# Layers 2 to 3 of a four-layer kernel: another order of the chains, moved gated adds, an earlier exp table, and seven spare products

## The chip, the cores and the metric

The kernel runs on one core of a Trainium2 chip. A core has five engines, each of which works through a queue of instructions of its own, in order: TensorE (PE in the profile; PEld is its weight loads), VectorE (DVE), ScalarE (ACT), GpSimd (POOL) and SyncE (SP, which here issues transfers). They meet through semaphores. The metric is the device time of one execution, in microseconds; lower is better. The profile calls a source line L477, for line 477 of the kernel.

## The reference, cut to what matters

Four layers work on a stream `x` of 4 x 256 tokens of 256 features. Each adds a gated cross attention to a small context and then a gated feed-forward part. The change lies where layer 2 ends and layer 3 begins:

```
x = x + tanh(g_xattn[2]) * L2_xattn(layernorm(x), ctx)     # 16 heads of 16, 64 keys, causal
x = x + tanh(g_ffn[2])   * L2_ffn(layernorm(x))            # int8-rounded x times int8-rounded weight
x = x + tanh(g_xattn[3]) * L3_xattn(layernorm(x), ctx)     # as in layer 2
x = x + tanh(g_ffn[3])   * L3_ffn(layernorm(x))            # shared experts + best 2 of 8

L2_ffn: x_max = max|x| of each token; x_scale = x_max/127; x_q = round(x/x_scale)
        y = (x_q @ w_q.T) * x_scale * w_scale + bias
attention: softmax(q k / 4, causal) v, then @ Wout.T
```

Everything is float32 but the rounded numbers, which are whole and go through TensorE as bfloat16.

## The kernel before, in words

`x` stays in SBUF as eight tiles of 128 tokens, `x[0]` to `x[7]`; tiles 0 to 3 are group 0, tiles 4 to 7 are group 1. Query products and feed-forward products take a group (512 tokens) at a time, softmax and its products a tile.

`layernorm(g)` takes the statistics of four tiles (`bn_stats` and `bn_aggr` on VectorE, L431 and L434), one square root on ScalarE (L436), a reciprocal on VectorE (L439), and scales the tiles: on VectorE (L450), or with `scalar=True` on ScalarE from a shift made at L443 (L447). The results come from the tag `xn` with seven buffers. `transposed` turns the four tiles on TensorE (L462) and copies the two halves out, one on ScalarE (L169) and one on VectorE (L171).

`attention23` is the attention of layers 2 and 3. `queries(g)` is normalisation, transposition and the query products (`mm2`, L477), which ScalarE scales into `xT` (L1034). It is run for group 0 first and, in steps, for group 1 beside the first tiles. For each tile, `scores` makes the products with the keys (L1048 for the causal mask in even tiles, L1058), the row maxima (L1071), the differences (L1073) and the exponentials (L1082); `weights` sums (L491), inverts (L492) and scales on GpSimd (L493); `attend` turns the weights (L507), copies them (L508), multiplies by the values (L1090), copies (L1099) and multiplies by the output weight (L1102). `in_flight` runs them as a pipeline: in iteration i the scores of tile i, the gated add of tile i-3, the weights of tile i-1 and `attend` of tile i-2. `gated_add` is one VectorE instruction, `x[t] = ps * gate + x[t]` (L512).

`ffn2` is the feed-forward part of layer 2. `rounded(g)` normalises a group on ScalarE, takes maxima (L1963), scales and rounds on VectorE (L1968, L1970), and adds the bias to `x` on GpSimd (L1974). `rounded(0)` is written into the last iterations of layer 2's attention. `ffn2` itself goes through the two groups: transposition (L1985), copies on ScalarE (L1986), products (L1991), then `y = ps * xs * scale` on VectorE (L1995) and `x[t] += y` on GpSimd (L1996). In the source `rounded(1)` comes ahead of group 0's products, and layer 3's `queries(0)` after all of `ffn2`.

The order of the work is not written out by hand. A planner takes the instructions by priority, which is the order of the source, and lays each engine's queue out beforehand from estimates of its own on when each would be ready; on the chip every engine then follows its queue. `behind(later, sooner)` forbids the planner to put one instruction ahead of another. Tiles of a tag share a number of buffers: `t4` has six of 4 KB, `xn` seven of 1 KB, `xT` two, the PSUM tag `mm` four.

ScalarE holds one table of functions at a time; square root and exponential need different ones, and a load (ACT_TABLE_LOAD in the profile) stands ahead of the first instruction that needs the other.

## Time and profile before

| what | value |
|---|---|
| median of 3 runs | 839.23 us (837.9 to 839.84) |
| the profiled execution, its own time | 837.3 us |
| its span, first to last instruction | 835.4 us |
| mean granted TensorE clock | 0.978 |
| busy: PE, DVE, ACT, POOL | 93%, 60%, 35%, 29% |
| layer 2's attention, first L1058 to end of last L1102 | 544.43 to 592.25 us |
| `ffn2`, first L1985 to end of last L1996 | 592.09 to 607.91 us |
| layer 3's attention, first L1058 to end of last L1102 | 615.53 to 661.34 us |

All times within the execution are microseconds from the start of its span. A busy TensorE is not one at its peak: matmuls overlap, and their ends are modelled. Idle time is given with the instruction that ended it.

### The profile page before, as it was taken

How to read it: one execution, taken by the hardware profiler on the slowest of the kernel's cores; microseconds unless marked ns; L12 is line 12 of the kernel's file. 1: busy time of each engine (PE TensorE's matmuls, PEld its weight loads, DVE VectorE, ACT ScalarE, POOL GpSimd, SP SyncE). 2: the span in 40 equal slices, each digit the busy share in tenths (PEclk: the TensorE clock that was granted, in tenths of full speed). 3: DMA queues.
4: the chain of work that ended last, by engine and by line, in shares of the span. 5: the costliest groups of instructions: out<-in, count | busy, mean ns of one | idle time of the engine just before them, and what ended most of it. 6: DMA issues, size and time to landing. Idle time of an engine off the chain costs nothing.

```text
span 835.4 us, 12470 instructions
## 1 busy us (share of the span) xinstructions
PE 772.9 (93%) x4492; PEld 519.2 (62%) x4492; DVE 497.3 (60%) x1146; ACT 291.6 (35%) x508; POOL 246.4 (29%) x211
## 2 busy tenths in 40 slices
PE   6999999898999999999999989998579899999993
PEld 4544443687575776676555746655236557999993
DVE  5565454874682554545879559788869664334320
ACT  2121112343312333322633477166455521233320
POOL 1355454322132343321031200024424203344222
PEclk9999999999999999999999999899789999999997
DMA  9510215700121253324900001800000102222223
GB/s 343 189 39 0 62 40 204 262 22 4 29 72 40 72 141 83 74 35 123 378 17 7 1 1 37 324 24 1 26 0 2 51 8 78 55 51 46 33 26 71
DMA packets 32740, 64.14 MB, mean 77 GB/s; under 512 B 5121, under 2 KB 19713, under 8 KB 31905
## 3 DMA queue, kind: packets, MB, share of 16 engines
q1 hardware_dynamic: 25216, 52.56, 18.2%
q0 software_dynamic: 7104, 9.93, 7.3%
q8 instruction: 39, 0.64, 0.3%
q10 hardware_dynamic: 352, 0.79, 0.3%
q14 instruction: 29, 0.23, 0.1%
HBM read 53.86 MB, written 10.45 MB: 77 GB/s over the span
## 4 chain that ended last, share of the span: by engine, by line
PE 51%; DVE 9%; ACT 4%; issue 1%; POOL 1%; DMA 0%; POOLq 0%; DVEq 0%; ACTq 0%
PE wide L1435 9%; PE wide L477 7%; PE mm L1451 4%; PE mm L1525 3%; PE mm L709 3%; PE mm L1899 3%; PE mm L1883 2%; PE wide L961 2%; PE wide L1562 2%; PE wide L1563 2%; PE mm L1774 2%; PE mm L477 2%; DVE sm L491 1%; PE mm L507 1%; PE mm L1102 1%; PE wide L1058 1%
## 5 line engine op out<-in xcount | busy, mean ns | idle before, releaser
L493 POOL TENSOR_TENSOR attn<-attn,sm 128x1024 f32<-128x1024 f32 x32 | 61.1, 1913 | 229.3 <-DVE sm L492 179.0
L477 PE MATMUL wide<-xT,big 128*128 128x512 f32 (+1 forms) x240 | 108.6, 600 | 1.1 <-DVE shared L1656 0.9
L737 DVE TENSOR_TENSOR rope<-wide,big 128x512 f32<-128x512 f32 x96 | 59.6, 682 | 52.0 <-PE wide L477 52.0
L477 PEld LDWEIGHTS wide<-xT,big 128*128 128x128 f32 (+1 forms) x240 | 43.4, 188 | 57.3 <-issue 49.3
L1435 PE MATMUL wide<-blk,still 128*128 128x128 f32 x640 | 74.8, 275 | 0.6 <-DVE blk L1407 0.6
L1435 PEld LDWEIGHTS wide<-blk,still 128*128 128x128 f32 x640 | 73.1, 192 | 0.8 <-issue 0.8
L709 PE MATMUL mm<-vo,attnT 128*128 128x256 f32 x256 | 58.6, 382 | 1.5 <-ACT attnT L508 1.5
L477 PE MATMUL wide<-xT,dense 128*128 128x512 f32 (+1 forms) x120 | 55.1, 599 | 0.0
L709 PEld LDWEIGHTS mm<-vo,attnT 128*128 128x128 f32 x256 | 47.8, 190 | 11.4 <-ACT attnT L508 3.2
L508 ACT COPY attnT<-mm 128x512 f32<-128x512 f32 x64 | 34.4, 587 | 46.2 <-PE mm L507 45.7
L491 DVE TENSOR_REDUCE sm<-attn 128x16 f32<-128x1024 f32 x32 | 38.7, 1208 | 15.2 <-ACT attn L485 13.8
L1397 DVE COPY still<-big 128x1024 f32 x20 | 13.9, 693 | 52.0 <-PE wide L1435 44.5
L1466 POOL DMA_INDIRECT sums<-ring,scratch x20 | 31.6, 1578 | 40.4 <-ACT ring L1462 18.8
L1466 POOL DMA_INDIRECT sums<-ring,big x17 | 27.0, 1591 | 48.5 <-ACT ring L1545 18.2
L507 PE MATMUL mm<-ident,attn 128*128 128x128 f32 x256 | 33.7, 275 | 5.7 <-POOL attn L493 5.7
L1370 POOL DMA_INDIRECT xs<-xd,scratch x20 | 20.0, 1002 | 62.3 <-PE mm L1404 34.0
L512 DVE SCALAR_TENSOR_TENSOR x<-mm,tg,x 128x256 f32<-128x256 f32 x44 | 20.5, 471 | 29.4 <-PE mm L709 18.2
L1451 PE MATMUL mm<-big,hidden 128*128 x160 | 37.7, 379 | 0.0
L507 PEld LDWEIGHTS mm<-ident,attn 128*128 128x128 f32 x256 | 29.1, 141 | 13.3 <-POOL attn L493 8.5
L1443 ACT ACTIVATE hidden<-wide 128x512 f32<-128x512 f32 x20 | 12.0, 599 | 72.8 <-PE wide L1435 67.5
L477 PEld LDWEIGHTS wide<-xT,dense 128*128 128x128 f32 (+1 forms) x120 | 21.5, 185 | 24.4 <-issue 22.7
L791 ACT COPY big<-mm 128x512 f32<-128x512 f32 x16 | 8.6, 589 | 68.0 <-PE mm L779 61.7
(359 smaller groups left out, 1572.1 us busy)
## 6 DMA issues: line engine op xcount, KB each, us to landing
big<-in_L_w_gate_up SPq DMA_DIRECT2D x8, 1024.0 KB, 12.1
big<-in_L_w_down SPq DMA_DIRECT2D x8, 512.0 KB, 8.9
w_L_qk<-in_L_qk SPq DMA_DIRECT2D x4, 896.0 KB
big<-in_L_w SPq DMA_DIRECT2D x2, 1480.0 KB, 7.9
big<-in_L_w SPq DMA_DIRECT2D x2, 1110.0 KB
big<-in_L_wo SPq DMA_DIRECT2D x1, 2048.0 KB
big<-in_L_w SPq DMA_DIRECT2D x2, 1024.0 KB, 5.3
xd<-xn SPq DMA_DIRECT2D x16, 128.0 KB, 1.8
```

Source lines behind the costliest of these rows:

```text
L477: nc.tensor.matmul(ps, w(c), xT[:, c, :], start=(c == 0), stop=(c == 1))
L491: nc.vector.tensor_reduce(sm, e, AX.X, ALU.add)
L493: nc.gpsimd.tensor_tensor(e, e, sm.unsqueeze(2).to_broadcast([P, groups, n]), ALU.mult)
L507: nc.tensor.transpose(ps[:, i * P : (i + 1) * P], ev[:, pr * P : (pr + 1) * P], ident)
L508: nc.scalar.copy(aT[:, half * 4 : half * 4 + 4, :].rearrange("p i t -> p (i t)"), ps)
L709: nc.tensor.matmul(ps[:, :D], aT[:, s, :], vo[:, s, :], start=(s == 0), stop=(s == NP - 1))
L737: nc.vector.tensor_tensor(m[:, s, :].rearrange("q (b t) -> q b t", t=S), ps[:, s, :].rearrange("q (b t) -> q b t", t=S), table, ALU.mult,)
L1435: nc.tensor.matmul(ps[:, k, f : f + P], w[:, at : at + P], st[:, c * P : (c + 1) * P], start=(c == 0), stop=(c == 1),)
L1451: nc.tensor.matmul(ps[:, :D], hT[:, j * P : (j + 1) * P], self.w[:, bass.ds(r + j * D, D)], start=(j == 0), stop=(j == n - 1),)
L1466: nc.gpsimd.indirect_dma_start(out=self.sums[b % len(self.sums)], out_offset=bass.IndirectOffsetOnAxis(ap=self.scatter[:, b : b + 1].bitca ...
L1525: nc.tensor.matmul(ps[:n, f : f + P], w[:, c * FU0 + f : c * FU0 + f + n], st[:, c * P : (c + 1) * P], start=(c == 0), stop=(c == 1),)
L1899: nc.tensor.matmul(ps[:, :D], terms[:, k, f, i * P : (i + 1) * P], w2[:, f, :], start=(f == 0 and k == 0), stop=(f == 7 and k == 2),)
```

## The change

- `ffn2` is written as `unit(g, xq, xs)`. Group 0's unit comes first; then seven products of `ident` with a weight of layer 3 (128x128 by 128x512, float32), whose result nothing reads, held behind group 0's last product; then layer 3's normalisation, transposition and query products of group 0; and only then `rounded(1)` and group 1's unit. `attention23` finds group 0's queries made.
- In layers 2 and 3, the gated adds of tiles 0 to 5 are a ScalarE multiplication into a tile of its own and a GpSimd add. Tiles 6 and 7 keep the VectorE instruction.
- In `attention23`, the table of the exponential is loaded right behind the square root of group 1.
- Layer 3's normalised tiles and the transposed rounded numbers come from the tag `t4` in place of `xn` and `xT`.

```
-    def layernorm(g, scalar=False, after=()):
+    def layernorm(g, scalar=False, after=(), into=None, table=None):
...
         made = nc.scalar.activation(rstd, mv[:, :, 1], AF.Sqrt, bias=eps)
         if after:
             behind(made, after[1])
+        if table is not None:
+            behind(nc.scalar.preload_act_table(table), made)
         nc.vector.reciprocal(rstd, rstd)
...
-            n = sb.tile([P, D], F32, tag="xn", name="xn", bufs=AHEAD + 2)
+            n = sb.tile([P, D], F32, tag="xn", name="xn", bufs=AHEAD + 2) if into is None else into[:, i, :]
...
-    def in_flight(scores, attend, gate, beside=iter(())):
+    def in_flight(scores, attend, gate, beside=iter(()), spared=0):
...
             if i >= 3:
-                gated_add(i - 3, outs.pop(i - 3)[:, :D], gate)
+                t, ps = i - 3, outs.pop(i - 3)[:, :D]
+                if t < spared:
+                    y = sb.tile([P, D], F32, tag="xn", name="y", bufs=AHEAD + 2)
+                    nc.scalar.mul(y, ps, gate)
+                    nc.gpsimd.tensor_tensor(x[t], x[t], y, ALU.add)
+                else:
+                    gated_add(t, ps, gate)
...
+    def head_queries(layer, xT):
+        w_q = loaded[f"L{layer}"][:, :512].rearrange("p (c o) -> p c o", c=2)
+        pss = [ps_mm() for _ in range(2)]
+        for half, ps in enumerate(pss):
+            mm2(ps, lambda c: w_q[:, c, half * P : (half + 1) * P], xT)
+        for half, ps in enumerate(pss):
+            nc.scalar.mul(xT[:, half, :], ps, 0.25)
+        return xT
...
         def queries(g):

-            xn = layernorm(g, layer == 3)
+            if (layer, g) in kept:
+                qT.append(kept.pop((layer, g)))
+                return
+            into = t4([P, TPG, D], "normal") if layer == 3 else None
+            xn = layernorm(g, layer == 3, into=into, table=AF.Exp if g else None)
             yield
             xT = transposed(xn)
             yield
...
+            qT.append(head_queries(layer, xT))
...
-        in_flight(scores, attend, gate, zip_longest(queries(1), beside))
+        in_flight(scores, attend, gate, zip_longest(queries(1), beside), NT - 2)
...
     def ffn2(gate):
         used("L2")
         wqT, scale, _ = kept["weights2"]
-        for g, (xq, xs) in enumerate([kept.pop("rounded"), rounded(1)]):
-            xqT = sb.tile([P, 2, TH], BF16, tag="xT", name="xT", bufs=2)
+
+        def unit(g, xq, xs):
+            xqT = t4([P, 1024], "xqT")[:, :TH].bitcast(BF16).rearrange("p (d t) -> p d t", d=2)
...
+            return made
+
+        last = unit(0, *kept.pop("rounded"))
+        ps = ps_mm()
+        for _ in range(7):
+            made = nc.tensor.matmul(ps, ident, loaded["L3"][:, :TH], start=True, stop=True)
+            behind(made, last)
+            last = made
+        normal = t4([P, TPG, D], "normal")
+        kept[3, 0] = head_queries(3, transposed(layernorm(0, True, into=normal)))
+        unit(1, *rounded(1))
```

More of the change, by code (lines that the diff above doesn't have):

```diff
@@ L1019, in attention23 @@
         w = loaded[f"L{layer}"]
-        w_q = w[:, :512].rearrange("p (c o) -> p c o", c=2)
         w_o = w[:, 512:1024].rearrange("p (c o) -> p c o", c=2)
@@ L1029, in queries @@
             yield
-            pss = [ps_mm() for _ in range(2)]
-            for half, ps in enumerate(pss):
-                mm2(ps, lambda c: w_q[:, c, half * P : (half + 1) * P], xT)
-            for half, ps in enumerate(pss):
-                nc.scalar.mul(xT[:, half, :], ps, 0.25)
-            qT.append(xT)
+            qT.append(head_queries(layer, xT))
         for _ in queries(0):
@@ L1990, in ffn2 @@
                 for d in range(2):
-                    nc.tensor.matmul(
+                    made = nc.tensor.matmul(
                         ps[:, :D], xqT[:, d, i * P : (i + 1) * P], wqT[:, d, :], start=(d == 0), stop=(d == 1)
```

## The prediction

> **What bounds the kernel now.** I first read the page's busy line and its 40 slices (20.9 us each; a digit is tenths of busy time, PEclk the granted TensorE clock).
>
> ```profile
> PE 772.9 (93%) x4492; PEld 519.2 (62%) x4492; DVE 497.3 (60%) x1146; ACT 291.6 (35%) x508; POOL 246.4 (29%) x211
> PE   6999999898999999999999989998579899999993
> ...
> PEclk9999999999999999999999999899789999999997
> ```
>
> TensorE bounds the kernel nearly everywhere. Busy and clock dip together in slices 29 and 30 (counted from 1), 585 to 627 us: where layer 2 ends and layer 3 begins. Next the table by stretch (us; busy and count of PE, PEld, DVE, ACT, POOL; PEclk; DMA).
>
> ```profile
> 548.00:578.00 30.00, 28.22 (x205) 16.07 (x202) 28.91 (x46) 20.56 (x40) 13.08 (x10) 1.00 0.00 1
> 578.00:594.00 16.00, 11.21 (x111) 7.38 (x107) 11.67 (x37) 10.01 (x20) 5.23 (x6) 1.00 0.02 4
> 594.00:610.00 16.00, 6.29 (x32) 3.17 (x29) 12.90 (x44) 6.42 (x15) 8.36 (x12) 0.58 0.09 30
> 610.00:626.00 16.00, 13.87 (x50) 6.55 (x50) 9.51 (x13) 8.56 (x13) 1.90 (x1) 0.89 0.00 0
> 626.00:642.00 16.00, 15.25 (x126) 9.98 (x127) 14.10 (x22) 8.13 (x13) 5.71 (x3) 0.89 0.01 1
> ```
>
> The hole is 594 to 610, around `ffn2`: TensorE works 6.29 of 16 us, at 0.58 of its clock. The timeline of each engine there (start, duration, work, then idle before it and its releaser):
>
> ```profile
> 593.72 1.21 PE L1991 MATMUL mm<-kept,xT 128*128 128x256 bf16 x8 [0.62 <-ACT xT L1986]
> 601.33 0.70 PE L1985 MATMUL mm<-ident,xn 128*128 128x128 bf16 x4 [6.40 <-DVE xn L1970]
> ...
> 603.43 1.89 PE L1991 MATMUL mm<-kept,xT 128*128 128x256 bf16 x8 [0.57 <-ACT xT L1986]
> 607.65 2.17 PE L462 MATMUL mm<-ident,xn 128*128 128x128 f32 x8 [2.33 <-ACT xn L447]
> 610.28 5.32 PE L477 MATMUL mm<-xT,w_L 128*128 128x512 f32 x8 [0.46 <-ACT xT L169]
> 615.53 1.46 PE L1058 MATMUL wide<-kbd,xT 64*128 64x256 f32 x8
> ```
> ```profile
> 596.32 0.47 DVE L1995 SCALAR_TENSOR_TENSOR y<-mm,xs,kept 128x256 f32<-128x256 f32 x1
> ...
> 604.51 1.66 DVE L1995 SCALAR_TENSOR_TENSOR y<-mm,xs,kept 128x256 f32<-128x256 f32 x4 [0.44 <-PE mm L1991]
> ...
> 617.03 1.22 DVE L1071 TENSOR_REDUCE mx<-wide 128x16 f32<-128x1024 f32 x1 [6.42 <-PE wide L1058]
> ```
> ```profile
> 607.00 2.08 ACT L447 ACTIVATE xn<-x,shift,rstd 128x256 f32<-128x256 f32 x4 [2.60 <-DVE st L431]
> ...
> 618.22 1.28 ACT L1082 ACT_TABLE_LOAD   x1
> ```
>
> Group 0's products are out at 594.93, but its first result is taken at 596.32, its layer 3 normalisation reaches ScalarE at 607.00 and its query products TensorE at 610.28, since group 1's rounding and result (604.51) stand ahead on VectorE. TensorE waits 6.40 us and then runs slowly. By one-us windows the clock is halved at 596.5, whole at 613.6, halved from 627.2 to 630.6.
>
> **The change, part by part.** The profiled execution took 837.3 us (span 835.4, 1.9 around it); the median is 839.23, so I put the sum against 837.3 and carry its difference to the median. All after 662 (PE-bound `ffn3`) is taken as moved whole.
>
> (1) Layer 2 attention. The exp load (549.16, 1.28) goes behind group 1's square root at 539.60, into ScalarE's idle 3.84 us before 543.74. The first exponential gains up to 1.28, but TensorE idles only 0.92 before the first L507 at 555.18: at most -0.9. Six gated adds leave VectorE (0.48 each, 2.9; it is busy 28.91 of 30) for ScalarE (0.48 each by the `mul` at L1676; 20.56 of 30 busy) and GpSimd (0.735 each by L1996, 4.4; 13.08 of 30 busy). TensorE is itself busy 28.22, so both together give at most 1.8. After 578 each tile is one chain L507, L508, L1090, L1099, L1102 of some 3.7 us through ScalarE; the two `mul`s there (tiles 4, 5) can stand ahead of a copy: 0 to +1.0. GpSimd's queue now holds adds that wait for L1102 and ScalarE ahead of the softmax products L493; those have slack (the product of tile 5 ends 575.75, its L507 starts 580.04), so 0. The tiles that move to the tag `t4` (six buffers) meet at most four live ones there; a wait for one would end with a tile's chain, inside the upper end. Taken -0.5, ends -1.8 and +1.0.
>
> (2) Group 0 ahead. No instruction or DMA is added here but the spares and the preload; SP's queue issues what it did. The second unit of before shows the chain's length: L1991 to its first y 1.08 (603.43 to 604.51); y to the end of four GpSimd adds 3.40 (607.91); on through statistics, root and reciprocal to 609.47, plus a shift of 0.15: 5.2 from the first y (the real shift ended 610.61, behind a 0.69 copy that won't be there). First xn to first L477: 3.28 (607.00 to 610.28). From 593.72: 593.72 + 1.08 + 5.2 + 0.1 + 3.28 = 603.4. VectorE also does group 1's rounding in between: four maxima of 0.42, and a GpSimd add beside it stretches VectorE's small ops (a 4-element shift took 1.80 us at 582.11 beside a GpSimd product; L1968 0.35 alone, 0.81 at most). I add 0.3: 603.7, against 610.28: -6.6. Ends: -7.5 (first y sooner at full clock) and -4.5 (maxima and one 1.8 stall ahead). GpSimd's bias adds and VectorE's rounding of group 1, now queued behind, are late next: term 4.
>
> (3) The spares and the clock. Seven products at 0.46 (3.70 for eight L477 at full clock, 619.01) cover 594.93 to 598.2; group 0's transposes start some 0.65 after its first xn, near 600.8. A hole of 2.6 us stays. If the spares themselves ran halved (0.91 each), they would end at 601.3, 0.5 late. The eight L477 took 5.32: 3.28 halved, 2.04 whole, which makes 0.91 each halved. Wholly fast is 3.70 (-1.6), wholly halved 7.3 (+2.0). Nearest row: TensorE idled 624.27 to 626.04, 1.77 us, and the clock halved from 627.2 for 3.4 us. So I expect one halved stretch touching part of L477: -0.4.
>
> The Trainium skill ("TensorE: Matmul & The Clock Gate", Part 1 and the HAM oscillation) has the clock fall after an idle window of about 3.4 us and warns of gaps above that. By it the 2.6 us hole would keep the clock, the term would be -1.6 and the sum -7.1; the 1.77 us row speaks against it, so the row decides.
>
> (4) Layer 3 attention up to the fourth L507 (642.47). Group 1's chain now runs beside it: on VectorE y 1.66, statistics 4 x 0.6, roots 0.3 = +4.4, less two gated adds 0.96, less VectorE's idle there (1.63 at 627.45 and 0.27) 1.9: +1.5. On TensorE L1985 1.3 and L1991 1.2, against 1.84 idle at 624.2 and some 1.7 of half clock at 627.2, either of which may come back. On ScalarE the preload 1.28 and four xn (2.08) can now stand ahead of the first exponential: up to +3.4. The load at 618.22 was hidden already (the exponential waited 0.58 more, for VectorE), so nothing is gained by it. Ends -1.7 (idle and half clock gone) and +3.4; VectorE is nearest to the limit, so near its 1.5: taken +1.2. Group 1's scores start 15.3 us after the first (630.82), so its delay has cover for that long.
>
> (5) The tail, 642 to 661: five tiles on the same serial chain; three `mul`s, 0 to +1.4, taken +0.4.
>
> Sum: -0.5 - 6.6 - 0.4 + 1.2 + 0.4 = -5.9: 831.4 for such an execution, 833.3 for the median. The ends add to -12.6 and +3.3.
>
> The skill ("GPSIMD Engine Reference", 4.1 Engine selection) puts elementwise adds of two tiles on VectorE and calls GpSimd about twice as slow. The rows agree on size (0.735 against 0.47); were all twelve moved adds on the path, (0.48 + 0.735 - 0.48) x 12 = 8.8 would turn the sum to +2.9; the table above has VectorE nearly full and GpSimd under half, so I price them at nothing.
>
> **Rivals.**
> A. Group 1 and the clock take most of it back: terms 3 and 4 at +0.8 and +3.4, sum -2.5: 836.7. For it: VectorE is busy 14.10 of 16 at 626 to 642. Against: it idles 6.42 before 617.03, which the moved work can fill.
> B. Clock whole throughout, first exponentials undelayed: -0.5 - 6.6 - 1.6 - 1.7 + 0.4 = -10.0: 829.2. Against: the 2.6 us hole.
> C. The change doesn't do what it says: queues are fixed ahead by a planner, and group 1's rounding, ready at 593.8, may still go first. Then about 839.2. Against: VectorE is idle 593.82 to 594.38, just when the first y becomes ready.
> D. Slower: on GpSimd's in-order queue each softmax product is put behind a gated add that waits for an older tile's L1102. Price 0.48 + 0.69 (four adds in 2.77) = 1.17 for each of 12 tiles, 14.0 - 5.9 = +8.1: 847.3. It decides where products end less than 1.17 us before their L507; at layer 2's tile 5 the room is 4.3. For it: tile 0's L507 in layer 3 waited 1.84 us for L493. Against: of the 16 groups of L507 only the first of each layer held TensorE up for it.
>
> **How the numbers follow.** Forecast 0.60, A 0.18, B 0.07, C 0.05, D 0.10. Own range of the forecast, three quarters of the half-widths of the terms' ends, added as squares (3.8): 830.4 to 836.2. The 8-in-10 range reaches up past A and down to B: 829.0 to 838.2; outside are C, D and part of B. 0.2% is 1.7 us, what a measurement here can tell: faster than 837.5 holds the forecast, B and 0.15 of A, 0.82; within, the rest of A and C, 0.08; slower, D, 0.10.
>
> **What would show it.** First y near 594.8; L477 of layer 3's first group near 603 and the first L1058 near 607 to 609, with group 1's unit after or beside them; a table load right behind each second-group root and none before the first exponentials; seven products of `ident` near 595; PEclk above 0.58 at 594 to 610. Wrong if two more table loads (2.6 us) appear because an exponential goes ahead of group 1's root, if first y stays near 596.3, or if the distance from first L1058 to fourth L507 (26.9) grows by over 3.

## The result: 0.92% slower

The changed kernel takes 846.12 us (844.17 to 849.04, 4 runs) beside 838.88 us of the kernel before (837.9 to 839.84, 4 runs): a ratio of 1.0092, interval 1.0066 to 1.0118. The forecast was 833.3 us.

The page of the changed kernel (span 847.1 us), busy line and slices:

```profile
PE 786.7 (93%) x4506; PEld 526.4 (62%) x4506; DVE 494.2 (58%) x1134; ACT 296.9 (35%) x520; POOL 254.6 (30%) x223
PE   6999999899999999999999989997868899999993
...
PEclk9999999999999999999999999899979999999997
```

The profiled execution (849.04 us) is the slowest of the four. TensorE's clock was lower in two stretches ahead of layer 2, at 460 to 470 and 490 to 500 (0.83 each), which the trace of before does not have there, and layer 2 starts 4.7 us later. So distances are compared, from the first transposition of layer 2 (537.00 before, 541.67 after). Leaving out the first and the last, the lowest slice of both PE and its clock is now the 30th, 614 to 635 us. The table by stretch, with the bounds of before's table moved by the same 4.67 us:

```profile
552.67:582.67 30.00, 26.53 (x187) 15.44 (x184) 26.07 (x42) 19.73 (x38) 13.84 (x12) 0.97 0.00 1
582.67:598.67 16.00, 11.97 (x105) 7.42 (x104) 8.05 (x16) 11.32 (x23) 8.08 (x9) 0.94 0.00 0
598.67:614.67 16.00, 13.99 (x65) 6.82 (x58) 11.64 (x42) 6.75 (x15) 5.64 (x9) 1.00 0.10 34
614.67:630.67 16.00, 9.37 (x53) 5.20 (x51) 13.29 (x32) 8.29 (x13) 3.32 (x5) 0.73 0.00 1
```

The hole at `ffn2` is filled (13.99 us busy where it was 6.29, clock 1.00 where it was 0.58), but some of that is the seven spare products, and a new hole has opened one stretch later (9.37 where it was 13.87). Layer 2's attention lost 1.7 us of TensorE's time in 30. By the prediction's own terms, in us:

| from | to | term | before | after | change | forecast |
|---|---|---|---|---|---|---|
| layer 2's first transposition | first product of `ffn2` | 1 | 56.72 | 60.83 | +4.1 | -0.5 |
| that | layer 3's first head product | 2 | 16.56 | 9.43 | -7.1 | -6.6 |
| that | layer 3's first scores | 3 | 5.25 | 3.63 | -1.6 | -0.4 |
| that | fourth turning of weights (L507, now L509) | 4 | 26.94 | 35.48 | +8.5 | +1.2 |
| that | first shared product of `ffn3` | 5 | 19.98 | 21.98 | +2.0 | +0.4 |
| sum | | | 125.45 | 131.35 | +5.9 | -5.9 |

The sum is as large as the one forecast, with the other sign; the medians differ by 7.2 us, and what follows these landmarks is 1.1 us longer in this execution (847.1 - 541.67 - 131.35 = 174.1 against 172.9).

In the changed kernel the lines have other numbers: scores L1073 (L1058 before), maxima L1086, differences L1088, exponential L1097, turning of the weights L509, their copy L510, context copy L1114, output product L1117, the scaled normal tiles L449, ScalarE's gate product L527 and GpSimd's add L528, spares L2018.

**Terms 2 and 3** came as forecast or better. TensorE's timeline:

```profile
603.91 6.28 PE L2018 MATMUL mm<-w_L,ident 128*128 128x512 f32 x14 [0.21 <-DVE y L2011]
...
611.93 3.70 PE L479 MATMUL mm<-xT,w_L 128*128 128x512 f32 x8 [0.24 <-ACT xT L169]
615.56 1.46 PE L1073 MATMUL wide<-kbd,xT 64*128 64x256 f32 x8
...
626.18 2.16 PE L464 MATMUL mm<-ident,normal 128*128 128x128 f32 x8 [6.57 <-ACT normal L449]
629.13 2.08 PE L1073 MATMUL wide<-kbd,xT 64*128 64x256 f32 x8
631.14 4.26 PE L479 MATMUL mm<-xT,w_L 128*128 128x512 f32 x8
635.24 1.04 PE L509 MATMUL mm<-ident,attn 128*128 128x128 f32 x8
```

The spares reach to group 0's transpositions, since seven of them last 6.28 us, and the eight head rows take 3.70 us (5.32 before). **Term 4** is the rest of this fence: TensorE waits 6.57 us, works on at half clock (0.50 granted from 624 to 632), and the first weights are turned 19.7 us after the first scores, where it was 10.5. VectorE's and ScalarE's timelines of that stretch:

```profile
618.68 1.23 DVE L1086 TENSOR_REDUCE mx<-wide 128x16 f32<-128x1024 f32 x1 [0.39 <-PE wide L1073]
619.82 1.65 DVE L2011 SCALAR_TENSOR_TENSOR y<-mm,xs,kept 128x256 f32<-128x256 f32 x4
...
624.54 2.48 DVE L1088 TENSOR_TENSOR attn<-wide,mx 128x512 f32<-128x512 f32 x4
```
```profile
624.24 1.28 ACT L440 ACT_TABLE_LOAD   x1
625.53 2.07 ACT L449 ACTIVATE normal<-x,shift,rstd 128x256 f32<-128x256 f32 x4
627.51 1.04 ACT L1097 ACTIVATE attn<-attn 128x1024 f32<-128x1024 f32 x1
```

The maxima of tiles 0 and 1 are ready, but group 1's results and statistics come next on VectorE, and the differences of both tiles start only at 624.54; on ScalarE the table and four scaled tiles stand ahead of the first exponential. In the kernel before, tile 0's differences followed its maxima, and the first weights had only the softmax product to wait for (VectorE, then TensorE):

```profile
618.77 1.28 DVE L1073 TENSOR_TENSOR attn<-wide,mx 128x512 f32<-128x512 f32 x2
```
```profile
626.04 1.09 PE L507 MATMUL mm<-ident,attn 128*128 128x128 f32 x8 [1.84 <-POOL attn L493]
```

**Term 1** is lost in layer 2's attention. First VectorE's lines, then TensorE's:

```profile
579.49 0.43 DVE L431 BATCH_NORM_STATS2 st<-x 128x6 f32<-128x256 f32 x1 [1.63 <-POOL x L528]
579.83 1.27 DVE L1088 TENSOR_TENSOR attn<-wide,mx 128x512 f32<-128x512 f32 x2
```
```profile
581.15 0.59 PE L1063 MATMUL wide<-causal,ident 128*128 128x512 bf16 x1 [1.72 <-DVE attn L1088]
581.53 1.91 PE L1117 MATMUL mm<-w_L,ctxTok 128*128 128x256 f32 x4
```

The statistics of `rounded(0)` wait for GpSimd's add and hold tile 6's differences behind them; TensorE idles 1.72 us and its clock halves (0.50 granted from 582 to 584): the four L1117 rows take 1.91 us, not 1.13. In the kernel before, the same statistics ran without a wait, and the differences right behind them:

```profile
576.39 0.37 DVE L431 BATCH_NORM_STATS2 st<-x 128x6 f32<-128x256 f32 x1
576.68 1.26 DVE L1073 TENSOR_TENSOR attn<-wide,mx 128x512 f32<-128x512 f32 x2
```

**Term 5**, layer 3's tail, is of the same kind. ScalarE, then TensorE:

```profile
660.29 1.28 ACT L436 ACT_TABLE_LOAD   x1
661.58 0.30 ACT L436 ACTIVATE rstd<-mv,eps 128x4 f32<-128x4 f32 x1
661.79 0.35 ACT L1114 COPY ctxTok<-mm 128x256 f32<-128x256 f32 x1
```
```profile
662.19 1.30 PE L1117 MATMUL mm<-w_L,ctxTok 128*128 128x256 f32 x4 [1.44 <-ACT ctxTok L1114]
663.29 1.91 PE L509 MATMUL mm<-ident,attn 128*128 128x128 f32 x8
```

In the kernel before, that table load (652.77) stood behind the copy.

### The profile page after: what moved, and what is told of

It is laid out like the page before. It is cut to its first block, busy times and chain, and to the rows that moved or that the text cites. A ratio compares the mean times of both kernels' runs of the same rounds, so it can differ in the third digit from the quotient of the medians.

```text
span 847.1 us, 12507 instructions
## 1 busy us (share of the span) xinstructions
PE 786.7 (93%) x4506; PEld 526.4 (62%) x4506; DVE 494.2 (58%) x1134; ACT 296.9 (35%) x520; POOL 254.6 (30%) x223
## 5 line engine op out<-in xcount | busy, mean ns | idle before, releaser
L495 POOL TENSOR_TENSOR attn<-attn,sm 128x1024 f32<-128x1024 f32 x32 | 61.1, 1911 | 214.3 <-DVE sm L494 193.2
L510 ACT COPY attnT<-mm 128x512 f32<-128x512 f32 x64 | 34.5, 588 | 41.1 <-PE mm L509 40.6
L1385 POOL DMA_INDIRECT xs<-xd,scratch x20 | 20.2, 1009 | 63.1 <-PE mm L1419 36.7
L509 PE MATMUL mm<-ident,attn 128*128 128x128 f32 x256 | 34.7, 280 | 3.5 <-POOL attn L495 3.5
L509 PEld LDWEIGHTS mm<-ident,attn 128*128 128x128 f32 x256 | 30.3, 144 | 12.3 <-POOL attn L495 5.6
L1458 ACT ACTIVATE hidden<-wide 128x512 f32<-128x512 f32 x20 | 12.0, 598 | 72.8 <-PE wide L1450 67.5
L753 POOL TENSOR_TENSOR rotated<-rope 128x512 f32<-128x512 f32 x12 | 15.3, 1273 | 58.4 <-DVE rope L745 58.4
L431 DVE BATCH_NORM_STATS2 st<-x 128x6 f32<-128x256 f32 x64 | 26.0, 414 | 11.1 <-POOL x L528 5.4
## 6 DMA issues: line engine op xcount, KB each, us to landing
xd<-xn SPq DMA_DIRECT2D x16, 128.0 KB, 1.9
```

The source lines that it names most:

```text
L431: made = nc.vector.bn_stats(st, x[g * TPG + i])
L495: nc.gpsimd.tensor_tensor(e, e, sm.unsqueeze(2).to_broadcast([P, groups, n]), ALU.mult)
L509: nc.tensor.transpose(ps[:, i * P : (i + 1) * P], ev[:, pr * P : (pr + 1) * P], ident)
L510: nc.scalar.copy(aT[:, half * 4 : half * 4 + 4, :].rearrange("p i t -> p (i t)"), ps)
L1385: nc.gpsimd.indirect_dma_start(out=xs, out_offset=None, in_=self.xd, in_offset=bass.IndirectOffsetOnAxis(ap=self.gather[:, b : b + 1].bitc ...
```

## The experiments

All distances in us from layer 2's first transposition, of the profiled execution; the ratio is to the kernel before on the same chip, with its 95% interval. "Scores to weights" is from layer 3's first scores to its first turned weights, "end" is the first shared product of `ffn3`. A distance is of one execution, and the clock varies between executions: nine traces of the old order have the same wait of 1.84 us ahead of layer 3's first weights (1.83 in one), and the second weights follow the first after 6.76 to 6.81 us in five of them (before among them, its clock halved) and after 5.23 or 5.24 in four. So 1.6 us in "end" can be the clock alone.

| kernel | first product of `ffn2` | first scores of layer 3 | scores to weights | end | ratio |
|---|---|---|---|---|---|
| before | 56.7 | 78.5 | 10.5 | 125.5 | 1 |
| changed | 60.8 | 73.9 | 19.7 | 131.4 | 1.0092 (1.0066 to 1.0118) |
| order_only | 57.1 | 70.1 | 17.9 | 126.6 | 1.0037 (1.0017 to 1.0057) |
| adds_only | 60.7 | 82.0 | 10.5 | 128.9 | 1.0078 (1.0053 to 1.0102) |
| after_xn | 61.6 | 74.7 | 19.7 | 131.5 | 1.0077 (1.0052 to 1.0102) |
| order_xn | 57.1 | 70.1 | 20.2 | 124.8 | 0.9999 (0.9981 to 1.0016) |
| adds2 | 61.8 | 84.4 | 10.5 | 130.1 | 1.0055 (1.0036 to 1.0074) |
| adds3 | 57.2 | 79.2 | 10.5 | 128.7 | 1.0026 (1.0004 to 1.0047) |
| adds2_late | 60.5 | 82.3 | 10.5 | 129.3 | 1.0052 (1.0031 to 1.0074) |
| adds2_dve | 60.1 | 81.9 | 10.5 | 128.8 | 1.0026 (1.0004 to 1.0048) |
| order_xn_no_spares | 57.2 | 72.8 | 16.8 | 126.1 | 0.9984 (0.9966 to 1.0002) |
| order_stats1 | 57.2 | 73.5 | 16.6 | 128.0 | 1.0010 (0.9989 to 1.0031) |
| order_late1 | 56.9 | 69.9 | 11.7 | 129.3 | 1.0054 (1.0031 to 1.0077) |
| order_late1b | 57.0 | 70.0 | 15.4 | 123.5 | 0.9980 (0.9956 to 1.0003) |
| order_late1c | 56.9 | 70.0 | 11.1 | 129.5 | 1.0069 (1.0045 to 1.0094) |
| order_xn_half | 56.9 | 71.6 | 17.0 | 124.1 | 0.9992 (0.9977 to 1.0007) |
| before_half | 56.7 | 77.5 | 10.5 | 123.1 | 0.9971 (0.9952 to 0.9990) |
| before_spares | 59.1 | 88.8 | 10.5 | 134.5 | 1.0075 (1.0052 to 1.0098) |
| before_spares52 | 56.7 | 78.4 | 10.5 | 125.4 | 0.9996 (0.9981 to 1.0010) |
| order_late1b_table | 56.9 | 69.9 | 15.4 | 123.7 | 0.9978 (0.9958 to 0.9999) |

### Which part costs

**order_only**: the new order, the spares and the tag `t4`, without moved adds and without the early table.

```
-        in_flight(scores, attend, gate, zip_longest(queries(1), beside), NT - 2)
+        in_flight(scores, attend, gate, zip_longest(queries(1), beside))
...
-            xn = layernorm(g, layer == 3, into=into, table=AF.Exp if g else None)
+            xn = layernorm(g, layer == 3, into=into)
```

> Only the new order of ffn2, the seven spare products and the tiles in t4; gated adds and the exp table as before. Theory (buffers and adds): two separate losses. In the trace of after, layer 3's first L1058 comes 8.8 us earlier against the end of layer 2's attention, but the first L507 gives 9.2 back, because tile 0's differences stand behind group 1's whole chain on VectorE; and the moved gated adds cost some 4 us in layer 2's attention and 1 to 2 us in layer 3's. So here the adds' part is gone and the other stays: 838 to 841, first L1058 to first L507 of layer 3 still near 19 us (10.5 before). Rival (order): the new order itself costs everything and the adds nothing: 846, as after.

**adds_only**: the twelve moved adds in the old order, old tags, no early table.

```
-        in_flight(scores, attend, gate, zip_longest(queries(1), beside))
+        in_flight(scores, attend, gate, zip_longest(queries(1), beside), NT - 2)
```

> The kernel before with nothing but the gated adds of tiles 0 to 5 of layers 2 and 3 moved to ScalarE and GpSimd. Theory (buffers and adds): VectorE's statistics of tile 2 wait at the head of its queue for GpSimd's add and hold tile 6's differences up; the distance from layer 2's first L1058 to its last L1102 grows by some 4 us, layer 3's by 1 to 2: 843 to 845. Rival (order): within 1 us of before, 838 to 840.

841.91 and 845.53 us beside 838.61, each just above the first theory's band: the order with the tag costs 0.37%, the adds alone 0.78%, together about what the whole change costs (0.92%). The profiled executions of these two, 839.38 and 840.79, are the fastest of their ten and six, so their distances show less than the ratios. The adds were priced at nothing and are the larger part. The order's gain at the first scores (8.5 us in order_only) is all lost behind them.

**after_xn** and **order_xn**: the changed kernel, and the order alone, with group 1's layer 3 tiles in the old tag `xn`.

```
-            into = t4([P, TPG, D], "normal") if layer == 3 else None
+            into = None
```

> The kernel after, but group 1's normalised tiles of layer 3 come from xn again, as before, not from t4; one line. Theory (buffers and adds): tiles of a tag are given out in the order of the source, so the differences of tile 0 (a t4 tile) can't be placed ahead of group 1's normalised tiles when those are t4 too; with xn they can, first L1058 to first L507 falls from 19.7 to about 11, and the time by 6 to 9 us: 837 to 840. Rival (order): group 1's chain is on the path wherever its tiles lie: within 2 us of after, 844 to 848.

> Both taken away: the new order with the spare products, gated adds and table as before, group 1's normalised tiles from xn. Theory (buffers and adds): what the prediction counted for the order alone is left, 5 to 8 us under before: 831 to 834. Rival (order): 844 to 848.

846.12 and 837.99 us: the first lies where the rival put it, the second between both forecasts. In the order alone the tag is worth the whole loss: order_xn is level with the kernel before, though not 5 to 8 us under it. Its VectorE takes tile 0's differences right behind tile 0's maxima (610.38 behind 609.13); in order_only they come behind group 1's results and statistics (616.81 behind 609.33). The tiles for scores and exponentials also come from `t4`, and group 1's normal tiles ask for a buffer there ahead of them in the source; that this is why the order changed is read from the two traces and the source. Nor do these differences explain the loss by themselves: the first weights come 2.3 us sooner after the scores in order_only, and it falls behind later, at a wait of 2.27 us for a context copy (645.23) with half clock after it. The cost of the tag is measured, its path is not shown. In the changed kernel the tag alone rescues nothing that these runs can tell: scores to weights stay at 19.7 us.

### Where the adds cost

**adds2**, **adds3**: the moved adds in layer 2 alone, in layer 3 alone.

```
+        in_flight(scores, attend, gate, zip_longest(queries(1), beside), NT - 2 if layer == 2 else 0)
```

> The kernel before with the six gated adds moved in layer 2's attention alone. adds_only took 845.5 against 838.6. Theory (queue heads): in layer 2 VectorE's statistics of tile 2 stand ahead of tile 6's differences and wait 1.63 us for GpSimd's add, TensorE idles 1.71 us behind them, and where such a gap falls the clock halves for 3.4 us more: most of the cost, 842 to 845. Rival (load): ScalarE and GpSimd are simply loaded more in both layers alike: half of it here, 841 to 843.

> The kernel before with the six gated adds moved in layer 3's attention alone. Theory (queue heads): here only the square root of the next part comes later, so that its table load stands ahead of tile 6's copy L1114 and TensorE idles 1.4 us: 839 to 841. Rival (load): half of the 6.9, 841 to 843.

0.55% and 0.26% sum to adds_only's 0.78%. Layer 2 reaches `ffn2` 5.1 us later in adds2, and in adds3 layer 3 takes 2.6 us longer from its first scores to the end (49.5 against 46.9). In adds_only that stretch is 46.9 as before, since its clock stayed whole behind the first weights and in the tail. The traces show the waits that the first theory named (in adds2 1.64 us on VectorE at 574.58 and 1.72 on TensorE at 576.25), but the times do not decide against even load: 842.55 and 842.35 us both lie in the rival's band of 841 to 843.

**adds2_late**: adds2 with the statistics of `rounded(0)` forbidden ahead of tile 7's differences, and their root ahead of its exponential.

```
-                kept["rounded"] = rounded(0)
+                kept["rounded"] = rounded(0, (kept["differences"], kept["exponentials"]))
```

> The six gated adds of layer 2's attention on ScalarE and GpSimd (as in the run adds2, which cost 4 us against the kernel before), and the statistics of the rounding that follows held behind tile 7's differences, their root behind tile 7's exponential. Theory 1 (the cost is the queue: the statistics stand at the head of VectorE's in-order queue, wait for GpSimd's adds, and hold the differences of tiles 6 and 7 behind them): most of the 4 us goes, the fourth to eighth context products follow each other as in the kernel before (about 4 us apart), and the time is 838 to 840 us. Theory 2 (the cost is GpSimd's and ScalarE's load or VectorE's slowing beside GpSimd): 841.5 to 843 us, as adds2.

843.03 beside 838.07 us: no better than adds2. The wait of 1.72 us is gone, and the fifth turning of weights comes 5.1 us after the fourth (7.4 in adds2, 4.9 before). But the next wait grows. ScalarE's root and its table load stand ahead of the copies of the sixth tile's turned weights here as in adds2, where TensorE waited 1.40 us (586.95); behind the held root the load (583.02, 1.28 us) begins 0.7 us later against that tile, TensorE waits 1.77 us and its clock halves:

```profile
585.14 0.91 PE L1105 MATMUL mm<-attnT,values 128*32 128x128 f32 x16 [1.77 <-ACT attnT L510]
586.60 1.42 PE L1117 MATMUL mm<-w_L,ctxTok 128*128 128x256 f32 x4 [0.55 <-ACT ctxTok L1114]
587.82 1.91 PE L509 MATMUL mm<-ident,attn 128*128 128x128 f32 x8
```

**adds2_dve**: adds2 with ScalarE's product kept and the add on VectorE.

```
-                    nc.gpsimd.tensor_tensor(x[t], x[t], y, ALU.add)
+                    nc.vector.tensor_tensor(x[t], x[t], y, ALU.add)
```

> As adds2 (six gated adds of layer 2's attention split, 4 us slower than the kernel before), with ScalarE's product of 0.47 us kept and the add given to VectorE instead of GpSimd. Theory 1 (the price is GpSimd's add: it stands behind the softmax product of 1.9 us in GpSimd's queue, and the statistics wait for it at the head of VectorE's): most of the price goes, layer 2's first shared-feed-forward product is 57 to 58.5 us after layer 2's first transposition (56.7 before, 61.8 in adds2), and the time is 838.5 to 840 us. Theory 2 (the price is ScalarE's product, which stands ahead of the next tile's copies out of PSUM in ScalarE's queue, in front of which TensorE then waits): 60 us or more after the first transposition, and 841 to 843 us.

841.91 beside 839.70 us, and `ffn2` is reached at 60.1, 3.3 us late: both numbers lie where the second theory put them, on ScalarE's product. But the ratio is half of adds2's, and in adds2 the delay was 5.1 us. So the product makes about half (by the ratios, whose intervals overlap) to two thirds (by the delays), the add on GpSimd the rest. Part of the 3.3 us is the halved clock after a wait of 1.40 us for a copy (L510, 582.89), with a table load (581.03, 1.28 us) and a product (582.53, 0.45 us) ahead of it.

### Where the order's gain goes

**order_xn_no_spares**: order_xn without the seven spares.

```
-        for _ in range(7):
+        for _ in range(0):
```

> order_xn without the seven spare products (838.0 with them). Theory (clock): TensorE then idles some 7 us ahead of group 0's transposes, the clock halves, and eight L477 take 5 to 7 us in place of 3.70; the first L1058 comes 1.5 to 3 us later and the time is 839.5 to 841. Rival (group 1's chain): what comes last after it is group 1's chain on VectorE, which the products don't touch: L477 is as slow, but the time stays within 1 us, 837 to 839.

838.38 beside 838.49 us, as the rival had it. The first scores come 2.6 us later than in order_xn, the end in the trace 1.3, and the time is no worse. So the first scores do not set the end in this order, and the 1.6 us of term 3 bought nothing that these runs can tell.

**order_stats1**: order_xn with group 1's normalisation written ahead of group 0's products.

```
+        second = layernorm(1, True)
         last = unit(0, *kept.pop("rounded"))
...
-        unit(1, *rounded(1))
+        unit(1, *rounded(1, second))
```

> order_xn with one thing more: group 1's normalisation for the rounding is written ahead of group 0's unit, its maxima and rounding stay behind. In order_xn its statistics start at 599.3, after all of group 0's, though VectorE idles 1.43 us at 594 with three of the four tiles ready: their small tiles (st, mv) come from tags that are given out in the order of the source. Theory (tag order): group 1's rounding is done some 5 us sooner, TensorE's wait of 5.85 us after the third L1058 group shrinks to 1 to 3: 833 to 835. Rival (VectorE full): VectorE is busy nearly without a break from 595 to 627, so group 0's chain is late by what group 1's gains: 837 to 839.

840.80 beside 838.49 us, a ratio that cannot be told from 1, with a median above both forecasts. Group 1's rounding comes some 3 us earlier, group 0's first head product 2.9 us later (69.4 against 66.5): what one group gains on VectorE the other pays.

The stretch itself, in order_xn. TensorE first, then VectorE's rows that TensorE waits behind:

```profile
619.23 2.08 PE L1073 MATMUL wide<-kbd,xT 64*128 64x256 f32 x8 [5.85 <-DVE shift L445]
621.24 2.01 PE L464 MATMUL mm<-ident,xn 128*128 128x128 f32 x8
...
623.89 4.13 PE L479 MATMUL mm<-xT,w_L 128*128 128x512 f32 x8
627.86 1.04 PE L509 MATMUL mm<-ident,attn 128*128 128x128 f32 x8
```
```profile
611.59 1.65 DVE L2011 SCALAR_TENSOR_TENSOR y<-mm,xs,kept 128x256 f32<-128x256 f32 x4
613.16 0.93 DVE L431 BATCH_NORM_STATS2 st<-x 128x6 f32<-128x256 f32 x2
...
617.74 0.68 DVE L1088 TENSOR_TENSOR attn<-wide,mx 128x512 f32<-128x512 f32 x1
```

Between tile 0's and tile 1's differences VectorE does group 1's results and statistics (from 611.59), then the next maxima and tile 0's sums; the fourth scores wait 5.85 us for tile 1's differences; then TensorE turns group 1's tiles and makes its head products, at half clock (0.50 granted from 619 to 624), ahead of the first weights. ScalarE loads a table three times there (610.54, 612.91, 617.07), since tile 0's exponential goes ahead of group 1's root: one of the signs of being wrong that the prediction had named, which the changed kernel itself does not show. From first scores to first weights (607.6 to 627.9) VectorE is busy 19.01 of 20.30 us; before it was 8.89 of 11.00 between 615 and 626.

**order_late1**, **order_late1b**: order_xn with group 1's rounding and unit, or its unit alone, moved to be the first steps beside layer 3's attention. The second:

```
-        unit(1, *rounded(1))
+        second = rounded(1)
+        def rest():
+            unit(1, *second)
+            yield
+        kept["second"] = rest()
...
-        in_flight(scores, attend, gate, zip_longest(queries(1), beside))
+        in_flight(scores, attend, gate, zip_longest(chain(kept.pop("second", ()), queries(1)), beside))
```

> The changed order alone (no gated adds moved, no early exp table, group 1's normalised tiles in their old buffers, as in the run order_xn), and in addition the second group's rounding and second group's products of the shared feed-forward part are written as the first two steps beside layer 3's attention instead of ahead of it, so that the first two context products stand ahead of group 1's transpositions and head products in TensorE's queue. In order_xn 19 to 20 us passed from the first scores to the first context product, where 10.5 passed in the kernel before. Theory 1 (group 0's attention is held up because group 1's chain stands ahead of it in the in-order queues): the stretch falls to 12 to 15 us, the first context product comes 5 us earlier than in order_xn, and the time is 832 to 836 us, below the kernel before. Theory 2 (VectorE has no free time in this stretch, so any order only hands the wait from one group to the other): the first context product comes earlier, but the later tiles' scores wait for group 1's chain, the last context product stays within 1.5 us of where it is, and the time is 837 to 840 us.

> As order_late1, but only the second group's products are moved into the attention; its rounding (statistics, maxima, scaled and rounded tiles on VectorE) stays ahead of layer 3. Theory 1 (queue order of TensorE is what holds the first context product): nearly all of order_late1's gain is here too, 833 to 836 us. Theory 2 (VectorE's load): 837 to 840 us, as order_xn.

842.41 and 836.48 beside 838.07 us. With both moved the first weights are turned after 11.7 us, almost as before, but the end is 4.5 us later than in order_xn: group 1's tiles are late. With the unit alone they come after 15.4 us and the end is 1.3 us earlier. order_late1 went beyond both forecasts, to the slow side; order_late1b lies between the two theories' bands.

**order_late1c**: the unit two steps further back, and one step less between group 1's transposition and its head products in layer 3.

```
             xT = transposed(xn)
-            yield
+            if layer == 2:
+                yield
             qT.append(head_queries(layer, xT))
...
         def rest():
+            yield
+            yield
             unit(1, *second)
             yield
```

> As order_late1b (836.5 us beside 838.1), with the second group's products moved two steps further into layer 3's attention, ahead of the third tile's scores rather than the first's, so that VectorE's differences of tile 1 stand ahead of the second group's results and statistics. In order_late1b TensorE waited 5.85 us ahead of the fourth tile's scores for these. Theory 1 (the order in VectorE's and ScalarE's queues decides): that wait shrinks to 2 to 4 us, the first context product comes 2 to 3 us earlier than the 15.4 us after the first scores, the fifth tile's scores come later by as much, and the time is 834.5 to 836.5 us. Theory 2 (VectorE is full, and any order gives the wait to the other group): the last context product does not move, 836 to 838.5 us.

843.57 beside 838.66 us, slower than either theory had it. The first two tiles' weights now come as early as in the kernel before (11.1 us), and then the third waits 16 us for the second group's chain:

```profile
619.64 1.09 PE L509 MATMUL mm<-ident,attn 128*128 128x128 f32 x8 [1.99 <-POOL attn L495]
624.24 1.09 PE L509 MATMUL mm<-ident,attn 128*128 128x128 f32 x8 [0.43 <-POOL attn L495]
...
630.42 0.66 PE L1106 MATMUL mm<-attnT,values 128*32 128x128 f32 x8 [4.38 <-ACT attnT L510]
...
640.59 1.09 PE L509 MATMUL mm<-ident,attn 128*128 128x128 f32 x8
```

The wait of 4.38 us is a third engine: between the two halves of a copy ScalarE loads the exponential's table (625.59, 1.28 us), after a load for group 1's root, and then scales four tiles (2.06 us). In these three runs moving the chain only chose which tile pays, and too far back it cost more than it saved.

**order_xn_half**, **before_half**: statistics of the second group's rounding and of layer 3's normalisations, and the second group's maxima, over 128 of the 256 columns, in the new order and in the old.

```
-            made = nc.vector.bn_stats(st, x[g * TPG + i])
+            made = nc.vector.bn_stats(st, x[g * TPG + i][:, :cols])
...
-            nc.vector.tensor_reduce(xs[:, i : i + 1], n, AX.X, ALU.max, apply_absolute_value=True)
+            nc.vector.tensor_reduce(xs[:, i : i + 1], n[:, : D // 2] if g else n, AX.X, ALU.max, apply_absolute_value=True)
```

> order_xn (the new order alone) with less work for VectorE in the crowded stretch: the statistics of the second group's rounding and of both groups' normalisation in layer 3, and the second group's maxima, are taken over the first 128 of the 256 columns. That is left out of the computation, and it takes some 2.5 to 3 us off VectorE between layer 2's last tiles and layer 3's fourth tile (12 statistics rows of 0.39 to 0.43 us and 4 maxima of 0.42 to 0.47 us, each about 40% shorter). Theory 1 (VectorE is the bound between the first scores and the first context product): first scores to first context product falls from 20.2 us to 17.5 to 18.5, and the time is 834.5 to 836 us. Theory 2 (what holds the first context product is where group 1's transpositions and head products stand in TensorE's queue, not VectorE's load): the first context product moves by less than 1 us, and the time stays at 837 to 838.5 us.

> The kernel before with the same statistics and maxima over half of the columns (this much is left out). It is the control of order_xn_half. Theory 1 (VectorE paces the new order, and in the old one only group 1's chain ahead of layer 3's first head products is on the path): the old order gains what lies ahead of its first head products, 1 to 1.8 us (4 statistics and 4 maxima of the rounding, 4 statistics of the normalisation), 836.5 to 837.5 us. Theory 2 (nothing of VectorE's load is on the path): within 0.1% of the kernel before.

836.75 and 836.77 beside 838.66 us; the second is where the first theory put it, the first lies between the two. The halved rows became a third shorter (statistics 0.43 to 0.29 us, maxima 0.42 to 0.28), some 2.2 us in all.

In the new order scores to weights fall by 3.3 us, but 1.4 of that is that the first scores come later; the first weights come 1.8 us earlier (88.5 against 90.4 from layer 2's first transposition) and the end 0.8. Nor does the saved work explain it: only four of the shortened statistics lie between the first scores and the first weights, and they end as they did (615.45 in both traces), since they wait for GpSimd's adds. What differs is the order that the planner laid. Tile 0's differences now stand behind group 1's statistics (615.45, in order_xn 610.38), and ScalarE loads a table once in the stretch, not three times. So this pair does not show that VectorE's load paces the stretch. At 644.12 TensorE waits 1.79 us for a context copy, which stands on ScalarE behind an exponential that waits for VectorE's differences.

In the old order the end comes 2.3 us earlier and the time falls by 0.29%. Of the 2.3 us, 1.1 lie ahead of layer 3's first head product, where the saved work stands; 1.6 are the clock, which stayed whole behind the first weights here (5.24 us to the second) and halved in before (6.81).

### The clock, and the best version

**before_spares**: the old order with 13 spares behind group 0's unit and 5 behind group 1's. **before_spares52**: 5 and 2.

```
+            ps = ps_mm()
+            for _ in range(2 if g else 5):
+                last = nc.tensor.matmul(ps, ident, loaded["L3"][:, :TH], start=True, stop=True)
+                behind(last, made)
+                made = last
```

> The kernel before with its own order, and spare products alone: 13 on TensorE after group 0's products of the shared feed-forward part and 5 after group 1's, in the two waits ahead of layer 3's first head products, which in the kernel before run at half the clock. Theory 1 (the halved clock there is on the path and the spare products, not the order, are what could gain): layer 3's first head products take 3.7 us rather than 5.6 to 5.8 and the time falls by 1.6 to 2.2 us, to 836.3 to 837 us. Theory 2 (what is gained there is taken back by the wait for VectorE behind it): within 0.2% of the kernel before, 837 to 840 us.

> The kernel before in its own order with spare products, five after group 0's products of the shared feed-forward part and two after group 1's: before_spares had 13 and 5, and its 13 products took 14.25 us, where the wait they stand in lasts 6.4 us, so that group 1's transpositions waited for them. Five take 4.5 to 5.5 us by that row and by the seven of the changed kernel (6.28 us), two take 1.8 to 2.2 us, and the wait there lasts 2.33 us. Theory 1 (the halved clock ahead of and in layer 3's first head products is on the path): the head products take 3.7 us instead of 5.32, and the time falls by 1 to 2.2 us, to 836 to 837.5 us. Theory 2 (VectorE's chain behind them takes it back): head products of 3.7 us, but the same distance to the shared products of layer 3 as before, 837.5 to 839 us.

844.77 beside 838.07, and 838.57 beside 839.70 us. The first is an error of size that shows what a filler costs when it is too long; the second fits the wait. TensorE in before_spares, then in before_spares52:

```profile
598.31 14.25 PE L1999 MATMUL mm<-w_L,ident 128*128 128x512 f32 x26 [1.91 <-DVE y L1995]
612.39 0.61 PE L1985 MATMUL mm<-ident,xn 128*128 128x128 bf16 x8
```
```profile
596.64 6.06 PE L1999 MATMUL mm<-w_L,ident 128*128 128x512 f32 x10 [1.91 <-DVE y L1995]
...
609.98 5.36 PE L477 MATMUL mm<-xT,w_L 128*128 128x512 f32 x8 [0.56 <-ACT xT L169]
```

Thirteen held group 1's transpositions to 612.39, though VectorE had finished their input at 603.87. That makes the way from the first product of `ffn2` to layer 3's first head product 9.5 us longer; another 2.4 us are a stretch of halved clock in layer 2 with no spares near it, and 2.9 come back in layer 3, 1.6 of them in head products of 3.70 us and 1.6 by a whole clock behind the first weights, as in before_half. Five and two gave full clock from 600 to 609.9, group 1's transpositions and products at full speed, and nothing at the end: behind them the wait was for VectorE and ScalarE. And the head products still took 5.36 us, since the clock halved anew at 609.9; what 3.70 would be worth in the old order by itself stays open.

**order_late1b_table**: order_late1b with the exponential's table loaded early.

```
-            xn = layernorm(g, layer == 3, into=into)
+            xn = layernorm(g, layer == 3, into=into, table=AF.Exp if g else None)
```

> order_late1b with the exp table loaded early, behind the root of the second group's normalisation in layers 2 and 3, and no gated adds moved. Theory 1 (in layer 2 the load of 1.28 us stands in front of the first exponential, and on the path): 0.4 us less in layer 2, nothing in layer 3, 835.8 to 836.5 us. Theory 2 (in layer 3 the load after the second group's root only changes places with the one that the next exponential brings): no difference from order_late1b that these rounds can tell, 836 to 837.5 us.

836.01 beside 838.66 us, within both theories' bands. The early table brings layer 2's first weights 0.33 us forward, which is gone at `ffn2` (56.93 against 56.97). This has the lowest ratio of the versions that compute all of the reference: 0.22% under the kernel before, by an interval that just leaves out 1, and not to be told from order_late1b's 0.20%.

## Why the prediction was wrong

Terms 2 and 3 hold: -8.8 together where -7.0 was forecast. Rival C, that nothing would be reordered, is out. D gave the right side for a wrong mechanism, and its 847.3 is near the measured 846.12 by luck: of the 16 groups of L509 in the changed kernel's two attentions only layer 2's first shows a wait for the softmax products L495 (0.56 us); what waited for GpSimd were VectorE's statistics, and TensorE waited for ScalarE's copies.

**The step that failed most is term 4**, +1.2 with an upper end of +3.4. It measured +8.5, so the sign that the prediction had set, that this distance grows by over 3, came; and it is +7.0 in order_xn, where neither adds nor table are in play. The step summed the moved work ("y 1.66, statistics 4 x 0.6, roots 0.3") and set it against VectorE's idle time, as a balance over the stretch. What decided was the place in the queue: that work stands between tile 0's and tile 1's differences, and group 1's turning and head products stand ahead of the first weights on TensorE. The prediction's argument against rival A, "it idles 6.42 before 617.03, which the moved work can fill", was true of before, where that idle was the wait for the late first scores; in the new order it is gone, because the first scores come earlier. VectorE is then busy 94% of the stretch (19.01 of 20.30). "Group 1's scores start 15.3 us after the first (630.82), so its delay has cover for that long" failed as well: its chain costs the other tiles, not its own.

The reason is shown as far as this: with group 1's chain moved out from in front of the first tiles, the first weights come 11.7 and 11.1 us after the first scores, nearly as in before (order_late1, order_late1c), and later tiles wait instead. So the chain's place in the queues makes the delay. How much of it is VectorE's and how much TensorE's own queue is not separated, since order_xn_half changed the order together with the work. Why the first weights, 1.3 us later in order_xn than in before counted from layer 2's first transposition, still give an end 0.6 us earlier was not tested either.

**Term 1**, "the two `mul`s there (tiles 4, 5) can stand ahead of a copy: 0 to +1.0", and of the moved adds "so I price them at nothing": +4.1. The room that was counted was GpSimd's share of the time and the slack of the softmax products. Who waits for the add's result was not followed: the statistics of `rounded(0)`, at the head of VectorE's queue, with differences behind them. adds2_late shows that ending this one wait is not enough, adds2_dve that ScalarE's product makes half of the delay or more and GpSimd's add the rest. The bound for all twelve adds on the path, 8.8 us, was the end that should have stayed in the range: adds_only cost 6.5 (0.78% of 838.6). What the Trainium skill, "GPSIMD Engine Reference", 4.1 Engine selection, advises, such adds on VectorE, is borne out here, by the waits more than by the add's own 0.73 against 0.48 us.

**Term 3** was mis-sized to the good: the prediction took 0.46 us for a spare product, which is one of the two rows that the profile counts for it. Seven last 6.28 us, so the hole of 2.6 us that it expected was not there, and its forecast of one halved stretch was not put to the test. The idle time in the row that it reasoned from is 1.84 us, not 1.77. order_xn_no_spares shows no gain in time from the spares.

**Term 5**: +2.0 for +0.4: a table load stands in front of a copy (660.29) and the clock halves behind it. The load stands there in adds3 (653.25) and also in order_xn (650.76), where no adds are moved, so either part of the change brings it. **Tag `t4`**: "a wait for one would end with a tile's chain, inside the upper end" was wrong by kind: with the tag VectorE takes the differences in another order, and order_only and order_xn differ by 0.38%.

**Rival A** had the direction of term 4 right, with too small a price, and term 3, which it put at +0.8, came as -1.6.

## What to carry to other kernels

When a chain is moved ahead, do not set its work against the receiving engine's idle time: that idle may be the very wait that is being removed. Write out the receiving queue instruction by instruction, and ask of each moved instruction what then stands behind it. An instruction moved to an idle engine is not free: price the wait of everything that needs its result, at the head of whichever in-order queue that is. A filler has to be shorter than the wait that it fills, at the clock that it will run at.

## What the runs showed of the hardware

A short idle of TensorE sometimes halved its clock for some 3.4 us, and sometimes not. After idle times of 1.72 us (changed kernel, 581.15), 1.77 us (adds2_late) and 1.40 us (adds2_dve) rows of 1.13 or 1.04 us soon took 1.91; after 1.40 us at 590.78 in the changed kernel and 1.79 us at 644.12 in order_xn_half they did not: TensorE's next rows took their usual 1.13 us. The plainest case is the wait of 1.84 us ahead of layer 3's first weights: in before the clock was halved behind it (0.50 granted from 628 to 630), in before_half it stayed whole (1.00 from 626 to 633). The Trainium skill, "TensorE: Matmul & The Clock Gate", Part 1, has the clock fall after an idle window of about 3.4 us, and has that window run freely, not reset by the kernel's start. The length of the slow stretches agrees with it; the idle time needed does not, and the measurement decides.

A spare product of 128x128 by 128x512 in float32 took 0.90 us in the changed kernel (6.28 for seven) and 1.10 us in before_spares (14.25 for thirteen), since some of them ran at half clock (0.50 granted from 598 to 604). In before_spares52, with 0.57 granted from 596 to 600, five took 6.06.
